# A two-layer graph network with routed experts: row terms turned by VectorE, layer-1 scaling on ScalarE, variance arithmetic on GpSimd, and another order within the steps

## The chip, the core and the metric

The kernel runs on one core of a Trainium2 chip. A core has five engines that work side by side, each through its own list of instructions in order: TensorE (PE in the profile; its weight loads are shown apart as PEld), VectorE (DVE), ScalarE (ACT), GpSimd (POOL) and SyncE (SP), which here only starts transfers. They meet through semaphores. TensorE writes into PSUM, which this kernel cuts into 8 banks of 512 fp32 values per partition; VectorE and ScalarE read PSUM and SBUF; the transfers with row indices (scatters) are started by GpSimd. The metric is the device time of one execution, in microseconds. Three runs of the kernel before gave a median of 1763.73 us (1761.31 to 1763.85).

## What is computed

There are 64 batches of 256 rows with 256 features, fp32 throughout, and one 256x256 adjacency that all batches share. Cut to what matters:

```python
x = x + elu(gat(layernorm(x), adj, W0, a0))       # 4 heads of 64, leaky slope 0.2
x = x + layernorm(x) @ Wf.T + bf
x = x + relu(gat(layernorm(x), adj, W1, a1))      # 1 head of 256, slope 0.01
t = layernorm(x)                                  # tokens
x = x + t + moe(t)                                # 8 experts, top 2, exact gelu, 256 -> 256 -> 256

def gat(h, adj, W, a):                            # per head
    q = h @ W
    e = leaky_relu(q @ a_src [rows] + q @ a_dst [columns])
    return softmax(where(adj, e, -big)) @ q
```

A batch therefore has four normalisations (call them norm 0, 1, 2 and 3: of the input, after layer 0's attention, after the linear layer, after layer 1's attention), two attentions, and a mixture of experts over all 16384 tokens.

## The kernel before, in words

**Attention without a softmax over scores.** The exponent of a leaky sum is written as a maximum of products, so one attention needs only, for each row, the exponentials of a few projected columns. `gnn_weights` (L139) widens the weight matrix by three columns per head: one for each of two terms along the keys and one for the term along the queries. `projected` (L322) multiplies the transposed input by that matrix (128x268 results for layer 0: 4 heads of 67; 128x259 for layer 1), lets ScalarE take `Exp` of the three columns with the row's 1/std as scale (L337), and lets VectorE scale the 64 (or 256) values of each head by 1/std and by one of the exponentials (L341). `scores` (L347) needs the query's term along the free axis of every partition: for each head and each half of the rows TensorE transposes a column that is broadcast to 128x128 (L353), which leaves the row term on all partitions of a PSUM tile `pd`. VectorE then forms `z = max(pd, key term) * mask` (L360). `attended` (L366) multiplies `z` by `q`, which has a column of sums at its end, and takes reciprocals.

**Normalisation.** `norm_stats` (L288) runs `bn_stats` and `bn_aggr` on VectorE for each half of a batch (L300, L301). `finish_norms` (L306) then makes 1/std on GpSimd in two instructions, an addition of eps (L308) and a power of -1/2 (L309). Two norms that fall into the same step share one pair of GpSimd instructions (tiles of 4 columns instead of 2).

**The order of the work.** The order is written out by a planner in the kernel (L909 to L942); nothing reorders it later. Every batch is a generator, `batch_layers` (L384), cut by `yield` into segments. A new batch begins every third step (`TICKS = 3`), and in each step every active batch issues one segment. Within a step the segments are issued by rank, lowest first; the rank of a segment is the number in the `yield` before it (or the one given to `begin`). So the work of one period (three steps, one new batch) holds one segment of every kind, each of another batch:

| step of the period | segments by rank, in the kernel before |
|---|---|
| first | relu of layer 1 (5), heads 2 and 3 of layer-0 scores (10), layer-1 projection (20), norm 1 and transposition (30), norm 0 and transposition of a new batch (40), tokens `xe` and `base` (50), second expert matmul `py`/`y` (80) |
| second | scaling of the experts' result (2), layer-1 scores (10), layer-0 projection (20), transposition of tokens (35), expert input `px` (40), layer-0 attention (50), norm 3 (60), linear layer and norm 2 (70), routing (75) |
| third | heads 0 and 1 of layer-0 scores (10), `by` from norm 3 (15), elu and residual (20), first expert matmul `ph` (30), layer-1 attention (40), router logits `pl` (50), transposition for layer 1 (60), routing (75) |

Norms 0 and 1 share GpSimd's two instructions in the first step ("finish A" below), norms 2 and 3 in the second ("finish B"). The order of issue is the order of every engine's list. All PSUM tiles come from one ring of 8 banks (`bank`, L78), so that no engine can be more than eight tiles ahead of the reader of the oldest.

**Experts.** Routing is done for chunks of four batches (later two and one): VectorE ranks tokens (`route`, L772), GpSimd sends each token's row to its two experts' regions in DRAM (L755, 4 indirect transfers per batch), and full pairs of 128 rows are loaded back, run through `expert_pair` (L598), and added into the output by GpSimd with accumulating indirect transfers (L695, 2 per pair, one pair per step, each waiting for the pair before it to land). In the middle of the run there are about two pairs per period; a period's pairs go 2, 2, 1, 3 over four batches. After the last batch the rest of the pairs and one batch done densely (`dense_expert`, L709) follow. Scatters and sends stand on GpSimd's list between finish A and finish B.

The lines in front of the change are these:

## Time and profile before

| what | value |
|---|---|
| median of three runs | 1763.73 us |
| the profiled execution | 1771.5 us, span 1769.8 us |
| TensorE busy (matmul) / weight loads | 1584.4 us (90%) / 1394.4 us (79%) |
| VectorE busy | 1296.0 us (73%) |
| ScalarE busy | 834.6 us (47%) |
| GpSimd busy | 838.8 us (47%) |
| mean granted TensorE clock | 0.957 |

A row of the profile's table of groups has the line, the engine, the operation, "output<-inputs", the number of instructions, the busy time, the mean duration, and the idle time of that engine just before them with the instruction that ended it. An fp32 matmul shows as two instructions. In the timeline a row has the start in us from the span's start, the duration, the engine, the line and the count of merged instructions; the bracket names an idle time before it and its releaser. Durations of neighbours overlap, since each includes the pipeline's tail: what an instruction takes from its engine is the distance between two starts. The starts of the linear layer's matmuls (L422), one group per batch, give the length of a period: 16.7 us where there is no expert work and no routing (from 113.6 us on, with longer ones between where a chunk is routed; 14 periods in the 263.8 us from 78.50 to 342.25 us), and a repeating 22.6, 23.5, 22, 26.1 us in the middle (43 periods in the 1023.3 us from 390.41 to 1413.73 us, 23.8 us each). The last 356 us hold two more periods and then experts alone.

The rows that the change touches, from the table of groups kept apart by shape:

| instruction | count | mean ns | busy us |
|---|---|---|---|
| L353 transposition of a broadcast column, PE | 640 | 280 | 105.3 |
| L341 scaling of `q`, 128x256, DVE | 256 | 479 | 112.6 |
| L300 `bn_stats`, DVE | 512 | 408 and 395 | 156.5 and 50.5 |
| L301 `bn_aggr`, DVE | 512 | 182 | 93.2 |
| L308 addition of eps, 128x4, POOL | 124 | 321 (median 228) | 39.7 |
| L309 power, 128x4 / 128x2, POOL | 124 / 8 | 1046 / 752 | 129.7 / 6.0 |

### The profile page before, as it was taken

To read this page: it belongs to the slowest core of one execution; us is meant where nothing else is said; L and a number is where in the kernel's file an instruction comes from. 1 tells how busy PE (TensorE), PEld (TensorE's weight loads), DVE (VectorE), ACT (ScalarE), POOL (GpSimd) and SP (SyncE) were. 2 spreads that over 40 slices of the span, in tenths; PEclk is the share of its full clock that TensorE was granted. 3 is DMA by queue.
4 is the path that set the end of the run, shared out by engine and by line. 5 is a ranking of instruction groups with operands and counts; after the bars stand their busy time and mean duration, and the time that the engine had idled before them with its cause. 6 is when DMAs were issued, how large, how long until landed. Compare 5 with 4: busy or idle time off the path is not lost. (4 is left out here: it accounts for less than half of the span.)

```text
span 1769.8 us, 29975 instructions
## 1 busy us (share of the span) xinstructions
PE 1584.4 (90%) x9254; PEld 1394.4 (79%) x9254; DVE 1296.0 (73%) x4808; ACT 834.6 (47%) x1773; POOL 838.8 (47%) x788
## 2 busy tenths in 40 slices
PE   5898889899999999999999999999999997688791
PEld 4777777688888888888888888888878886577681
DVE  6888888978787888878787878788888777422231
ACT  1232324255555555555555555555555565433340
POOL 0111333426555464646464646465664555634444
PEclk9999999999999999999999999999999898898896
DMA  3510112135545353544444444445453545665753
GB/s 101 173 37 24 54 50 68 53 108 116 131 111 134 90 127 101 126 115 123 118 110 123 94 118 111 130 111 136 116 133 84 111 120 133 173 180 96 172 110 42
DMA packets 137372, 192.89 MB, mean 109 GB/s; under 512 B 18680, under 2 KB 91392, under 8 KB 137216
## 3 DMA queue, kind: packets, MB, share of 16 engines
q1 hardware_dynamic: 86592, 122.61, 22.3%
q0 software_dynamic: 49632, 67.39, 20.7%
q8 instruction: 76, 1.25, 0.3%
q10 hardware_dynamic: 992, 0.99, 0.2%
q14 instruction: 80, 0.66, 0.1%
HBM read 101.77 MB, written 89.15 MB: 108 GB/s over the span
## 5 line engine op out<-in xcount | busy, mean ns | idle before, releaser
L695 POOL DMA_INDIRECT out_dram<-y,to x262 | 418.9, 1599 | 325.7 <-DMA out_dram<-y,to 150.1
L374 PE MATMUL pv<-q,z 128*128 128x65 f32 (+1 forms) x2560 | 366.3, 298 | 8.0 <-DVE y L684 8.0
L374 PEld LDWEIGHTS pv<-q,z 128*128 128x128 f32 x2560 | 337.2, 195 | 23.4 <-DVE y L684 10.0
L329 PE MATMUL pq<-wx,xT 128*128 128x268 f32 (+1 forms) x1024 | 269.2, 407 | 35.2 <-ACT xT L319 35.2
L663 PE MATMUL ph<-sT,we 128*128 128x256 f32 x1048 | 250.6, 395 | 46.3 <-ACT sT L635 25.5
L308 POOL TENSOR_SCALAR rstd<-mv 128x4 f32<-128x4 f32 (+1 forms) x132 | 43.4, 329 | 518.0 <-DVE mv L301 450.0
L755 POOL DMA_INDIRECT xs<-xng,pos x248 | 250.7, 1011 | 69.1 <-issue 67.7
L360 DVE SCALAR_TENSOR_TENSOR z<-pd,q,mask 128x256 f32<-128x256 f32 x640 | 265.1, 473 | 6.5 <-PE pd L353 6.3
L678 PE MATMUL py<-w2s,hT 128*128 (+1 forms) x1176 | 264.1, 380 | 0.6 <-ACT hT L669 0.6
L663 PEld LDWEIGHTS ph<-sT,we 128*128 128x128 f32 x1048 | 204.2, 200 | 76.1 <-ACT sT L635 27.1
L329 PEld LDWEIGHTS pq<-wx,xT 128*128 128x128 f32 x1024 | 191.0, 197 | 84.1 <-ACT xT L319 56.3
L678 PEld LDWEIGHTS py<-w2s,hT 128*128 128x128 f32 x1176 | 219.6, 190 | 28.6 <-ACT hT L669 1.0
L319 ACT COPY xT<-pt 128x512 f32<-128x512 f32 x256 | 143.6, 591 | 173.5 <-PE pt L315 173.5
L684 DVE TENSOR_TENSOR y<-py,b2s 128x512 f32<-128x512 f32 x147 | 97.3, 688 | 143.4 <-PE py L678 86.7
L656 ACT ACTIVATE y<-y,w 128x256 f32<-128x256 f32 x262 | 113.5, 498 | 187.9 <-DVE y L684 187.9
L669 ACT ACTIVATE hT<-ph,we 128x256 f32<-128x256 f32 x294 | 123.2, 470 | 164.6 <-PE ph L663 124.1
L341 DVE SCALAR_TENSOR_TENSOR q<-pq,rstd,q 128x256 f32<-128x256 f32 x256 | 112.6, 479 | 77.1 <-ACT q L337 76.9
L300 DVE BATCH_NORM_STATS2 stats<-x 128x6 f32<-128x256 f32 x384 | 156.5, 408 | 2.2
L309 POOL TENSOR_TENSOR rstd<-rstd,mhalf 128x4 f32<-128x4 f32 (+1 forms) x132 | 135.7, 1028 | 10.9
L422 PE MATMUL pf<-wfT,xT 128*128 128x256 f32 x512 | 132.0, 403 | 0.0
L353 PE MATMUL pd<-ident,q 128*128 128x128 f32 x640 | 105.3, 280 | 10.5 <-ACT q L337 10.5
L408 ACT ACTIVATE e<-hp 128x512 f32<-128x512 f32 x64 | 40.3, 630 | 155.9 <-DVE hp L402 155.9
(147 smaller groups left out, 2107.4 us busy)
## 6 DMA issues: line engine op xcount, KB each, us to landing
we<-wpack SPq DMA_DIRECT2D x147, 288.0 KB, 5.6
xr<-xs SPq DMA_DIRECT2D x131, 260.0 KB, 3.6
xin<-in_x_dram SPq DMA_DIRECT2D x64, 256.0 KB, 4.4
out_dram<-base SPq DMA_DIRECT2D x64, 256.0 KB, 3.4
out_dram<-y,to POOLq DMA_INDIRECT x262, 3.9
xs<-xng,pos POOLq DMA_INDIRECT x248, 2.6
xs<-fill SPq DMA_DIRECT2D x9, 260.0 KB, 5.0
wpack<-wt SPq DMA_DIRECT2D x8, 288.0 KB, 2.8
```

The costliest lines, as they stand in the source:

```text
L300: nc.vector.bn_stats(stats[:, t, :], src[:, t, :])
L309: nc.gpsimd.tensor_tensor(rstd[:, :n], rstd[:, :n], mhalf[:, :n], ALU.pow)
L319: nc.scalar.copy(dst, pt)
L329: nc.tensor.matmul(pq.rearrange("p h c -> p (h c)"), xT[:, k, t * P : (t + 1) * P], wx[:, k, :], start=(k == 0), stop=(k == KT - 1),)
L360: nc.vector.scalar_tensor_tensor(z[:, j, :], pd[:, i, :], q[:, j, h, d + 2 : d + 3], mask[:, j, :], op0=ALU.max, op1=ALU.mult,)
L374: nc.tensor.matmul(pv[:, h, :], z[:, j, t * P : (t + 1) * P], q[:, j, h, : d + 1], start=(j == 0), stop=(j == NT - 1),)
L422: nc.tensor.matmul(pf[:, t, :], xT[:, k, t * P : (t + 1) * P], wfT[:, k, :], start=(k == 0), stop=(k == KT - 1),)
L663: nc.tensor.matmul(ph[:, f, :], we[:, k * D + f * P : k * D + (f + 1) * P], xT[:, k, :], start=(k == 0), stop=(k == KT - 1),)
L669: nc.scalar.activation(hT[:, f, :], ph[:, f, :], AF.Gelu, bias=we[:, C_B1 + f : C_B1 + f + 1])
L678: nc.tensor.matmul(py[:, t, :], hT[:, f, t * P : (t + 1) * P], w2s[:, e, f * D : (f + 1) * D].rearrange("p e c -> p (e c)"), start=(f == 0 ...
L695: d = nc.gpsimd.indirect_dma_start(out=out_rows, out_offset=bass.IndirectOffsetOnAxis(ap=to[:, t : t + 1], axis=0), in_=y[:, t, :], in_off ...
L755: d = nc.gpsimd.indirect_dma_start(out=xs_d[: E * CAP * PAIR, :], out_offset=bass.IndirectOffsetOnAxis(ap=at, axis=0), in_=xe, in_offset=None,
```

## The change

There are four edits.

1. **Row terms of layer 0.** TensorE's eight transpositions per batch go. In the segment of the projection VectorE spreads each row's term over four columns, one per block of 32 partitions, with a mask `quad` (`quadrants`); in the third step one matmul with a constant `peers` (its ones join partitions with the same place in their block of 32) puts, on every partition, the term of the row at the same place of each block (`shared`, PSUM tile `pr`), and VectorE copies that to SBUF (`rs`). VectorE then transposes in blocks of 32x32 from `rs`, broadcast 32 times, straight into the PSUM tile `pd` (128x512, one instruction per two heads). The rest of `scores` is as before. Layer 1 keeps its two transpositions.
2. **Layer 1's projection.** `projected1` and `scores1` take the place of `projected` and `scores`: ScalarE scales the values (two `Copy` with the row's 1/std, out of PSUM), and multiplies the mask by the key's exponential (two `Copy` of 128x256, tile `me`), which VectorE then uses in place of the mask.
3. **Statistics.** VectorE's `bn_aggr` goes. GpSimd makes the variance from the even and odd halves of `bn_stats`: seven instructions instead of two in each finish, and an eighth for the doubled mean in the second step's.
4. **Order.** The new batch's segment gets rank 15 instead of 40, layer 1's projection 40 instead of 20, and `by` 45 instead of 15. On TensorE the first step then runs: transposition of the input, transposition after norm 1, layer-1 projection. Four work tiles lose their second buffer.

```diff
+    G = P // S                                   # S = 32
+    quad = const.tile([P, G], F32, tag="quad", name="quad")
+    nc.vector.tensor_reduce(quad, ident.rearrange("p (g a) -> p g a", a=S), AX.X, ALU.add)
+    peers = const.tile([P, G, S], F32, tag="peers", name="peers")
...
     def norm_stats(src):
...
-            nc.vector.bn_stats(stats[:, t, :], src[:, t, :])
-            nc.vector.bn_aggr(mv[:, at + t, :], stats[:, t, :])
+            nc.vector.bn_stats(stats[:, at + t, :], src[:, t, :])
...
     def finish_norms(n):
-        nc.gpsimd.tensor_scalar_add(rstd[:, :n], mv[:, :n, 1], EPS)
-        nc.gpsimd.tensor_tensor(rstd[:, :n], rstd[:, :n], mhalf[:, :n], ALU.pow)
+        nc.gpsimd.tensor_tensor(diff, stats[:, :, 1], stats[:, :, 4], ALU.subtract)
+        nc.gpsimd.tensor_tensor(rstd, stats[:, :, 2], stats[:, :, 5], ALU.add)
+        nc.gpsimd.tensor_tensor(diff, diff, diff, ALU.mult)
+        nc.gpsimd.tensor_scalar(diff, diff, D / 4.0, None, op0=ALU.mult)
+        nc.gpsimd.tensor_tensor(rstd, rstd, diff, ALU.add)
+        nc.gpsimd.tensor_scalar(rstd, rstd, 1.0 / D, EPS, op0=ALU.mult, op1=ALU.add)
+        nc.gpsimd.tensor_tensor(rstd, rstd, mhalf[:, :n], ALU.pow)
+        if (len(order_steps) - 1) % TICKS == 1:
+            nc.gpsimd.tensor_tensor(means, stats[:, :, 1], stats[:, :, 4], ALU.add)
...
+    def projected1(xT, rstd, b):
...
+        for t, pq in enumerate(pqs):
+            nc.scalar.activation(ex[:, t, :], pq[:, D:], AF.Exp, scale=rstd[:, t : t + 1])
+            nc.scalar.activation(q[:, t, :D], pq[:, :D], AF.Copy, scale=rstd[:, t : t + 1])
+        for j in range(NT):
+            nc.scalar.activation(me[:, j, :], masks[1][:, j, :], AF.Copy, scale=ex[:, j, 0:1])
...
+    def quadrants(q):
+        nc.vector.tensor_tensor(rq, <q's row terms, broadcast to G>, <quad, broadcast>, ALU.mult)
...
+    def shared(rq):
+        nc.tensor.matmul(pr, peers, rq, start=True, stop=True)      # 128x128 by 128x32
+        nc.vector.tensor_copy(rs, pr)
...
     def scores(q, heads, hs, mask, probs, rs=None):
+        if rs is not None:
+            nc.vector.transpose(pd, rs[:, heads of hs, :, None].to_broadcast([P, 2, NT * G, S]))
-        for i, h in enumerate(hs):
+        for i, h in enumerate(hs if rs is None else ()):
             ...transpositions by TensorE...
...
-        yield 20
-        q = projected(xT, wx1, 1, rstd)
+        yield 40
+        q, ex, me = projected1(xT, rstd, b)
...
-        yield 15
+        yield 45
         by = ...
...
-                    begin(nxt, 40)
+                    begin(nxt, 15)
```

## The prediction, as it was put on record

> **What bounds the kernel now.** The page comes first: engine totals, and the busy tenths of 40 slices.
>
> ```profile
> PE 1584.4 (90%) x9254; PEld 1394.4 (79%) x9254; DVE 1296.0 (73%) x4808; ACT 834.6 (47%) x1773; POOL 838.8 (47%) x788
> ...
> PE   5898889899999999999999999999999997688791
> ...
> DVE  6888888978787888878787878788888777422231
> ```
>
> TensorE is full from slice 8 to slice 32, but not in slices 2 to 7, where VectorE stands as high; so I read two stretches apart, by busy time per window (PE, PEld, DVE, ACT, POOL).
>
> ```profile
> 78.50:342.25 263.75, 229.19 (x1399) 196.24 (x1398) 228.95 (x809) 90.85 (x217) 70.48 (x89) 0.95 0.15 47
> ...
> 390.41:1413.73 1023.32, 988.95 (x5989) 883.66 (x5988) 837.69 (x3092) 566.04 (x1175) 573.24 (x526) 0.98 0.47 115
> ```
>
> The middle holds 43 periods of 23.8 us; TensorE works 23.0 of them (97%), VectorE 19.5, ScalarE 13.2, GpSimd 13.3. It is bound by TensorE's work. What stalls it, from the waits of TensorE between 400 and 1300 us (38 periods):
>
> ```profile
> PE pq L329 <- ACT xT L319: 15.2, 45, 0.6
> PE pv L374 <- DVE y L684: 6.4, 10, 0.7
> PE px L631 <- DMA xr<-xs: 5.9, 5, 2.2
> ```
>
> So 0.4 us per period is the layer-1 projection, which waits for a transposed tile that ScalarE is still copying. The early stretch (14 periods) differs: both engines are at 87%. One of its periods, TensorE:
>
> ```profile
> 208.63 0.60 PE L353 MATMUL pd<-ident,q 128*128 128x128 f32 x4
> 209.07 1.90 PE L374 MATMUL pv<-q,z 128*128 128x257 f32 x8
> 210.81 0.95 PE L489 MATMUL pl<-rT,xT 128*128 128x8 f32 x8
> 211.62 0.63 PE L315 MATMUL pt<-ident,x 128*128 128x128 f32 x4
> 212.09 0.60 PE L353 MATMUL pd<-ident,q 128*128 128x128 f32 x4
> 212.98 2.02 PE L329 MATMUL pq<-wx,xT 128*128 128x259 f32 x8 [0.29 <-ACT xT L319]
> ```
>
> and the next one's VectorE, GpSimd and ScalarE:
>
> ```profile
> 219.55 0.39 DVE L300 BATCH_NORM_STATS2 stats<-xin 128x6 f32<-128x256 f32 x1
> 219.98 0.18 DVE L301 BATCH_NORM_AGGREGATE mv<-stats 128x2 f32<-128x6 f32 x1
> 220.08 0.84 DVE L360 SCALAR_TENSOR_TENSOR z<-pd,q,mask 128x256 f32<-128x256 f32 x2
> 222.02 0.88 DVE L341 SCALAR_TENSOR_TENSOR q<-pq,rstd,q 128x256 f32<-128x256 f32 x2 [1.10 <-ACT q L337]
> ...
> 220.33 0.23 POOL L308 TENSOR_SCALAR rstd<-mv 128x4 f32<-128x4 f32 x1 [2.21 <-DVE mv L301]
> 220.64 1.04 POOL L309 TENSOR_TENSOR rstd<-rstd,mhalf 128x4 f32<-128x4 f32 x1
> ...
> 221.71 0.43 ACT L337 ACTIVATE q<-pq,rstd 128x12 f32<-128x12 f32 x2 [2.07 <-POOL rstd L309]
> ```
>
> VectorE idles 1.1 us there: the chain statistics, finish A on GpSimd, ScalarE's `Exp`, scaling of `q` has nothing behind it. Whatever makes finish A longer lengthens this period.
>
> **The change, part by part**, per batch (one period), costs as distances between starts.
>
> *TensorE.* Four transpositions take 0.44 us (208.63 to 209.07), so the eight removed are worth 0.88. The `peers` matmul (128x32, two passes) is nearest to `pl`: eight passes in 0.81 us, 0.10 each, so 0.2; between 0.2 and the 0.47 of two 128x268 passes. Net 0.66 less. `pr` stands directly after `pf`, where the first transpositions stood, but needs VectorE's scaling and mask (0.88 + 0.2 us) beyond `Exp`. In the middle this is covered: TensorE has token transposition, `px`, 3.5 us of layer-0 `pv` and 1.8 us of `pf` in between.
>
> *Order on TensorE.* The input's transposition and norm 1's (0.44 each) now stand between the layer-1 transposition and its projection, where 0.44 us of removed `pd` stood. The 0.4 us wait goes. The new batch's segment also issues the load of a later input; on SyncE's list it keeps its place, and on GpSimd's list no scatter or send changes sides with a finish. `by` moves behind layer 1's reciprocals, so that the longer finish B is waited for by nothing else on VectorE. Late next is layer 1's own `pd`: it waits for `Exp`, which on ScalarE now stands behind two copies `xT` (1.07 us in the middle's rows) and a scaling (0.42), on VectorE behind the extra work before layer 1's reciprocals. Its cover is `py`, 1.73 us per expert pair. With two or three pairs that holds; with one (a quarter of the periods) I expect about 1 us of wait, 0.25 per period.
>
> *VectorE.* Removed: layer 1's scaling, 0.78 (217.16 to 217.94 in that period); eight `bn_aggr`. A half of a batch now takes 0.53 us with aggregation; statistics alone should space like other 256-wide instructions (four `z` in 1.57 us, 0.39 each), 0.14 less, 1.1 per batch; at most 1.46 (the 93.2 us of L301 over 64). Added: two block transpositions of 128x512. No row shows this operation. Nearest are the 512-wide copy out of PSUM (L127, 684 ns) and addition into SBUF (L684, 688 ns): I take 0.69 each; below by two 128x256 at 0.39, no gain; above by twice the row, 1.38. `rq` and `rs` are small tiles (L786, 128x64 from PSUM, 192 ns): 0.2 each. Sum 1.78 - 0.78 - 1.1 = -0.1: VectorE's load stays.
>
> The Trainium skill's page "VectorE: DVE Perf Modes", section "The three transpose paths", speaks against this edit: it gives VectorE 311 ns for 128x128 in bf16, in 32x32 blocks only, and SBUF as the target. By that, as an estimate, four times 311 ns make 1.24 us per instruction, 1.1 us more per batch than my row, some 15 us over the early stretch; no run here shows it yet.
>
> *ScalarE.* Two scalings out of PSUM (like L445, a pair in 0.84) and two of the mask (like L656, four in 1.71): 1.7 us more on 13.2 of 23.8. The number of table loads in its list is unchanged. Alone it binds nothing; its place ahead of tokens delays layer 0's `Exp` by about as much as VectorE's experts' results already do.
>
> *GpSimd.* Per finish five more instructions, an eighth in B: eleven per period. A `tensor_scalar` on 128x4 starts the next 0.31 us later (220.33 to 220.64). The others are two-input instructions; their only row is the power, 752 ns on two columns and 1046 on four, which leaves 0.46 fixed, 0.54 with the gap. So 0.31 to 0.54: finish A grows by 1.55 to 2.5 us, a period by 3.4 to 5.9. I take 0.31 to 0.35, as additions are nearer to the addition than to a power. With its 0.3 us issue gaps GpSimd stands at 15.1 of 23.8, so at 18.5 to 21. Queued behind a finish are a period's four sends and the scatters; they lose idle time (450 us were spent waiting for statistics), and the experts' rows are needed a whole step later.
>
> The Trainium skill's "GPSIMD Engine Reference" (section "Elementwise — side-by-side cycle accounting") holds GpSimd about half as fast as VectorE for two-input work. Against it: here eight `bn_aggr` cost VectorE 1.1 us of spacing, and eleven GpSimd instructions cost 3.4 us of an engine that is 56% busy. By the rule statistics belong on VectorE, and the sum would be 20 us better early and about 1 us per period tighter in the middle.
>
> *Early stretch.* VectorE's order there is statistics, layer 1's two `z` (0.84), scaling of `q`. From the end of statistics to the scaling: finish A 2.9 to 3.7, `Exp` and hand-overs 0.5, less the 0.84. Against 1.1 before, idle time grows by 1.55 to 2.5, work shrinks by 0.1. So +1.4 per period, 14 periods, +20 us (at most +35; nothing, if ScalarE's new work and GpSimd's overlap better than I read). TensorE's removed work gives nothing here.
>
> *Middle.* VectorE 19.4, plus the wait for finish A behind results (1.3) and `z` (0.84), 1.2 to 2.0: about 21, under TensorE's 22.3. So TensorE stays the bound: -0.66 - 0.40 + 0.25 = -0.81 on 47 periods (43 and two at either end): -38 us.
>
> *Rest.* `quad` and `peers` are five small instructions in the set-up, under 1 us each: at most +1, among waits for weights. The smaller rings: each of the tiles is read out within two steps, and written once per three; nothing. The last 310 us (chain of waits: experts' matmuls and scatters that wait for each other) hold no edited instruction: 0.
>
> Sum: +20 - 38 + 1 = -17. The profiled execution took 1771.5 us, 0.4% over the median; 1754 for it, and 1746 for the median of runs. A measurement of this kernel can tell about 0.2%, 3.5 us.
>
> **Rivals.**
>
> *The vector chain takes the bound in the middle (slower).* If the block transposition costs 1.24 us or more, or GpSimd's instructions space at 0.54, VectorE's 21 becomes 22.1 to 23.5 and routing (10.6 us of VectorE instructions per four batches, unevenly placed) no longer fits. From 23.8 per period the middle gains nothing; early +1.4 to +2.5 remains. For it: VectorE's 82% plus a wait that lengthens. Against: over 4 us between 19.5 and 23.8 now. 1764 + 20 to 35: about 1785.
>
> *The early loss does not come.* If finish A's chain is hidden (statistics of the input now come first, and short GpSimd instructions may run closer than 0.31), only the middle counts: 1764 - 38 = 1726; with every stall gone too (0.8 + 0.66 on 47) 1695. Against it: the 1.1 us wait with GpSimd as releaser, 14 times.
>
> *Nothing moves.* TensorE's freed time turns into waits for the ring of 8 banks (`pv` already waits for `y`, and `pr` is one tile more): the middle gains 0.4, 1764 - 19 + 20 = 1765.
>
> **How the numbers follow.** Forecast (1730 to 1757): 0.37. No early loss (1695 to 1730): 0.27. Nothing moves (within 0.2%): 0.08. Vector chain (1768 to 1800): 0.28. Faster is the first two, 0.62 rounded down for the edge; slower 0.30. The range for 8 in 10 is 1708 to 1788; the forecast's own is 1730 to 1757.
>
> **What would show it.** Right: no L353-like row but the two layer-1 transpositions; block transposition near 0.69 us; GpSimd's small instructions near 0.3; middle periods near 23.0; early plain periods near 18.1 with VectorE waiting over 2 us for `Exp`; TensorE's wait for `xT` gone from the middle and a shorter one for layer 1's `Exp`. Wrong: a block transposition above 1.2 us, finish A above 4 us, TensorE below 92% in the middle, or early periods at 16.7.

## The result, and the profile after

The changed kernel takes 1821.97 us (median; 1809.02 to 1826.34), the kernel before beside it 1763.79 (1761.31 to 1768.47): a ratio of 1.0314, 95% interval 1.0254 to 1.0374. It is 3.1% slower, where 1746 us was forecast. The profiled execution took 1826.34 us, span 1824.6, to be set against the 1771.5 and 1769.8 of before.

The page of the changed kernel, engine totals and the busy tenths of 40 slices:

```profile
PE 1572.9 (86%) x8870; PEld 1382.3 (76%) x8870; DVE 1268.8 (70%) x4429; ACT 933.8 (51%) x2029; POOL 1007.8 (55%) x1516
...
PE   5888778789898989899999999899989987787792
...
DVE  6777888867678777868786868788778875422221
...
PEclk9889888889899999999999999999989999788896
```

All work that was to shrink did: TensorE has 384 instructions fewer, VectorE is busy 27 us less. But TensorE's slices 8 to 32, a row of nines before, now have eights among them, and the granted clock shows eights in the early slices, where it showed nines. The two stretches by themselves, same periods as before (14 early, 43 in the middle), busy time per window (PE, PEld, DVE, ACT, POOL, then the granted clock):

```profile
85.92:366.19 280.27, 228.76 (x1314) 197.35 (x1314) 224.55 (x725) 113.83 (x273) 106.07 (x244) 0.88 0.14 44
420.05:1460.27 1040.22, 968.66 (x5731) 863.46 (x5730) 815.25 (x2830) 630.72 (x1346) 683.46 (x997) 0.98 0.46 113
```

| stage, profiled execution | before | after | difference |
|---|---|---|---|
| start to the third linear layer | 78.5 | 85.9 | +7.4 |
| early, 14 periods | 263.8 (18.84 each) | 280.3 (20.02) | +16.5 |
| between | 48.2 | 53.9 | +5.7 |
| middle, 43 periods | 1023.3 (23.80 each) | 1040.2 (24.19) | +16.9 |
| rest | 356.1 | 364.3 | +8.3 |

No single stage carries the loss. Dividing a window's busy time by its periods gives two splits that the rest of this text uses. Early, VectorE was busy 16.36 us of a period and idle 2.49; it is now busy 16.04 and idle 3.98. In the middle TensorE was busy 23.00 and idle 0.80; it is now busy 22.53 and idle 1.66. TensorE did lose 0.47 us of work per period there, and waits 0.86 us more. What it waits for, in the middle window of the kernel before (total us, number, longest):

```profile
PE pq L329 <- ACT xT L319: 17.0, 50, 0.6
...
PE pv L374 <- DVE y L684: 8.0, 11, 1.6
...
PE px L631 <- DMA xr<-xs: 6.5, 6, 2.2
```

and in that of the changed kernel, with VectorE's longest wait above them:

```profile
DVE q L362 <- ACT q L358: 106.4, 43, 7.1
...
PE pt L336 <- DVE x L503: 27.7, 22, 2.4
...
PE pq L350 <- DVE z L449: 18.5, 11, 2.5
PE px L721 <- DMA xr<-xs: 17.9, 19, 2.4
```

The wait for `xT` is gone, as the new order promised. In its place TensorE waits for VectorE's residual `x1` (norm 1's transposition, 0.64 us per period), for a bank whose reader is VectorE's `z` (0.43), and longer for the experts' rows (0.42 after 0.15). VectorE's wait for layer 0's `Exp` has gone from 51.1 us in this stretch to 106.4.

**An early period.** TensorE, then VectorE, in the timeline of the changed kernel:

```profile
207.78 0.60 PE L336 MATMUL pt<-ident,xin 128*128 128x128 f32 x4
212.06 0.91 PE L336 MATMUL pt<-ident,x 128*128 128x128 f32 x4 [3.69 <-DVE x L503]
212.76 3.36 PE L382 MATMUL pq<-wx,xT 128*128 128x259 f32 x8
...
218.88 3.68 PE L463 MATMUL pv<-q,z 128*128 128x65 f32 x32
```

```profile
208.09 0.73 DVE L436 STREAM_TRANSPOSE pd<-rs 128x512 f32<-128x512 f32 x1
208.86 1.66 DVE L449 SCALAR_TENSOR_TENSOR z<-pd,q,mask 128x256 f32<-128x256 f32 x4
...
211.22 0.69 DVE L503 SCALAR_TENSOR_TENSOR x<-e,x 128x512 f32<-128x512 f32 x1
...
219.73 0.88 DVE L362 SCALAR_TENSOR_TENSOR q<-pq,rstd,q 128x256 f32<-128x256 f32 x2 [1.64 <-ACT q L358]
...
222.61 0.18 DVE L470 RECIPROCAL rinv<-pv 128x4 f32<-128x4 f32 x1 [1.60 <-PE pv L463]
```

TensorE waits 3.69 us for `x1`; then the layer-1 projection, which took 2.02 us in each of the 14 early periods before, takes 3.36 (3.1 to 3.7 in 12 of the 14 now); then VectorE waits for the `pv` behind it. Each waits for the other once per period, so a period is VectorE's work plus its waits. The two waits over the whole early stretch, in the kernel before and in the changed kernel:

```profile
DVE q L341 <- ACT q L337: 14.1, 14, 1.1
PE pt L315 <- DVE x L412: 13.4, 6, 3.5
...
PE pt L336 <- DVE x L503: 44.4, 14, 5.7
...
DVE q L362 <- ACT q L358: 25.3, 13, 2.9
```

**A middle period.** GpSimd's list from finish B to finish A in the changed kernel:

```profile
1049.89 0.20 POOL L321 TENSOR_TENSOR diff<-stats 128x4 f32<-128x4 f32 x1 [1.58 <-DVE rs L428]
...
1052.39 0.62 POOL L330 TENSOR_TENSOR double<-stats 128x4 f32<-128x4 f32 x1
1053.17 1.55 POOL L845 DMA_INDIRECT xs<-xng,pos  x1 [0.17 <-issue]
...
1060.75 1.58 POOL L785 DMA_INDIRECT out_dram<-y,to  x1 [0.30 <-ACT xng L553]
1061.77 0.80 POOL L321 TENSOR_TENSOR diff<-stats 128x4 f32<-128x4 f32 x1
...
1063.83 1.04 POOL L328 TENSOR_TENSOR rstd<-rstd,mhalf 128x4 f32<-128x4 f32 x1
```

and VectorE beside it:

```profile
1057.74 0.74 DVE L311 BATCH_NORM_STATS2 stats<-x 128x6 f32<-128x256 f32 x2
...
1065.21 0.88 DVE L362 SCALAR_TENSOR_TENSOR q<-pq,rstd,q 128x256 f32<-128x256 f32 x2 [5.05 <-ACT q L358]
```

The statistics for finish A are there at 1058.5, but GpSimd reaches them only at 1061.77: between the two finishes it has four sends and two scatters and no idle time but the gap at each issue. VectorE stands for 5.05 us. The counterpart before has the same four sends and two scatters, ends them at 972.2 and has 1.42 us to spare:

```profile
961.95 0.23 POOL L308 TENSOR_SCALAR rstd<-mv 128x4 f32<-128x4 f32 x1 [12.26 <-DVE mv L301]
962.26 1.04 POOL L309 TENSOR_TENSOR rstd<-rstd,mhalf 128x4 f32<-128x4 f32 x1
...
970.60 1.60 POOL L695 DMA_INDIRECT out_dram<-y,to  x1 [0.30 <-issue]
973.62 0.22 POOL L308 TENSOR_SCALAR rstd<-mv 128x4 f32<-128x4 f32 x1 [1.42 <-DVE mv L301]
```

The two periods are not quite alike: in the one before VectorE also routes tokens ahead of these statistics (some 3 us, from 965.98 to 968.96), in the changed kernel's it does not. The mean over all 43 middle periods says the same without this. From the end of its last statistics to the first instruction of finish A it takes 0.30 us in the kernel before (over 0.3 us in 10 periods) and 1.66 us in the changed kernel (in 31); finish A itself takes 1.53 and 3.07 us there. In the early stretch, where there are few sends, the delay is 0.15 and 0.10 us, and finish A takes 1.34 and 2.54.

### The profile page after: what moved, and what is told of

It is laid out like the page before. It is cut to its first block, busy times and chain, and to the rows that moved or that the text cites. A ratio compares the mean times of both kernels' runs of the same rounds, so it can differ in the third digit from the quotient of the medians.

```text
span 1824.6 us, 29624 instructions
## 1 busy us (share of the span) xinstructions
PE 1572.9 (86%) x8870; PEld 1382.3 (76%) x8870; DVE 1268.8 (70%) x4429; ACT 933.8 (51%) x2029; POOL 1007.8 (55%) x1516
## 5 line engine op out<-in xcount | busy, mean ns | idle before, releaser
L845 POOL DMA_INDIRECT xs<-xng,pos x248 | 265.1, 1069 | 67.6 <-issue 66.7
L753 PE MATMUL ph<-sT,we 128*128 128x256 f32 x1048 | 254.9, 400 | 42.3 <-ACT sT L725 21.6
L321 POOL TENSOR_TENSOR diff<-stats 128x4 f32<-128x4 f32 (+1 forms) x132 | 59.0, 447 | 383.3 <-DVE stats L311 309.3
L449 DVE SCALAR_TENSOR_TENSOR z<-pd,q,mask 128x256 f32<-128x256 f32 x512 | 212.4, 478 | 4.5
L336 PE MATMUL pt<-ident,x 128*128 128x128 f32 x512 | 88.5, 300 | 88.3 <-DVE x L503 87.6
L362 DVE SCALAR_TENSOR_TENSOR q<-pq,rstd,q 128x256 f32<-128x256 f32 x128 | 56.3, 481 | 147.7 <-ACT q L358 147.7
L382 PE MATMUL pq<-wx,xT 128*128 128x259 f32 x512 | 156.8, 460 | 0.9 <-ACT xT L340 0.9
L350 PE MATMUL pq<-wx,xT 128*128 128x268 f32 x512 | 133.5, 402 | 19.9 <-DVE z L449 18.5
L311 DVE BATCH_NORM_STATS2 stats<-x 128x6 f32<-128x256 f32 x384 | 142.7, 414 | 2.2
L336 PEld LDWEIGHTS pt<-ident,x 128*128 128x128 f32 x512 | 64.9, 160 | 98.2 <-issue 52.1
```

The lines of the kernel that those rows point to most:

```text
L311: nc.vector.bn_stats(stats[:, at + t, :], src[:, t, :])
L336: nc.tensor.transpose(pt[:, k, t * P : (t + 1) * P], src[:, t, k * P : (k + 1) * P], ident)
L350: nc.tensor.matmul(pq.rearrange("p h c -> p (h c)"), xT[:, k, t * P : (t + 1) * P], wx[:, k, :], start=(k == 0), stop=(k == KT - 1),)
L382: nc.tensor.matmul(pq, xT[:, k, t * P : (t + 1) * P], wx1[:, k, :], start=(k == 0), stop=(k == KT - 1),)
L449: nc.vector.scalar_tensor_tensor(z[:, j, :], pd[:, i, :], q[:, j, h, d + 2 : d + 3], mask[:, j, :], op0=ALU.max, op1=ALU.mult,)
L753: nc.tensor.matmul(ph[:, f, :], we[:, k * D + f * P : k * D + (f + 1) * P], xT[:, k, :], start=(k == 0), stop=(k == KT - 1),)
```

## The experiments

Every ratio is against the kernel before on the same chip, with its 95% interval. Waits, periods and busy times are from each kernel's profiled execution; the kernel before differs by 1.0% between the chips (medians 1764 to 1781 us), so microseconds of different runs are compared roughly. "Delay of finish A" is the mean time from its last statistics to its first instruction in the 43 middle periods.

### One edit undone

**proj20**: the layer-1 projection goes back in front of the two transpositions.

```diff
-        yield 40
+        yield 20
         q, ex, me = projected1(xT, rstd, b)
```

> The changed kernel, with one rank put back: layer 1's projection at 20 instead of 40, so that TensorE runs it between the input's transposition and norm 1's transposition. Theory 'order' (TensorE stalls because norm 1's transposition now stands ahead of the projection and meets VectorE's residual x1 too early, 87.6 us of waits against 18.8 before, and works at a lower clock after each stall): the waits for x1 fall below 30 us and the time to 1745 to 1775. Theory 'GpSimd' (finish A is late because GpSimd's list is longer, VectorE waits 147.7 us for layer 0's Exp against 76.9): the waits for x1 may fall, but VectorE's waits stay near 150 us and the time at 1805 or more.

Measured: 1.0436 [1.0332, 1.0539]. The wait for `x1` leaves the top of TensorE's list, and that for a bank that `z` reads grows from 18.5 to 25.3 us, `xT` returns with 14.1, and the experts' rows stay (27.6 after 29.2). Early periods are 19.97 us, middle ones 24.56 instead of 24.19, with less idle time (1.45 after 1.66) but TensorE busy 23.12 instead of 22.53, at a granted clock of 0.96 instead of 0.98. That the new rank is what made the kernel slow falls.

**order_back**: all three ranks as before.

```diff
-                    begin(nxt, 15)
+                    begin(nxt, 40)
...
-        yield 40            # layer-1 projection
+        yield 20
...
-        yield 45            # by
+        yield 15
```

> The changed kernel with all three ranks as before (40, 20, 15); the other three edits stay. 'Order': 1755 to 1785, a little slower than with one rank put back, since the projection's wait for the copied tile (15 to 20 us in all) returns and `by` now waits for finish B on VectorE. 'GpSimd': 1810 to 1850, since the norms of the input are again taken after norm 1 and `by` waits for a finish B that is 2 us longer.

Measured: 1.0387 [1.0312, 1.0463]; early periods 21.31 us instead of 20.02, the start 93.7 us instead of 85.9. Beside the other edits the new order is not what costs; that it gains there is not shown, since the two intervals overlap.

**aggr_back**: `bn_aggr` on VectorE and finishes of two GpSimd instructions again.

```diff
-            nc.vector.bn_stats(stats[:, at + t, :], src[:, t, :])
+            nc.vector.bn_stats(stats[:, t, :], src[:, t, :])
+            nc.vector.bn_aggr(mv[:, at + t, :], stats[:, t, :])
...
-        nc.gpsimd.tensor_tensor(diff, stats[:, :, 1], stats[:, :, 4], ALU.subtract)
-        ...seven more...
+        nc.gpsimd.tensor_scalar_add(rstd[:, :n], mv[:, :n, 1], EPS)
+        nc.gpsimd.tensor_tensor(rstd[:, :n], rstd[:, :n], mhalf[:, :n], ALU.pow)
```

> The changed kernel with the aggregation back on VectorE and the two-instruction finish on GpSimd; the other edits stay. 'GpSimd': VectorE's wait for layer 0's Exp falls from 147.7 to about 80 us, the time to 1765 to 1790. 'Order': VectorE has 1.1 us more per period ahead of x1, TensorE's waits for x1 stay at 87 us or grow, the time is 1815 to 1850.

Measured: 1.0137 [1.0065, 1.0209], 1.7% less than the changed kernel. The waits of the whole run:

```profile
PE pt L326 <- DVE x L493: 90.7, 40, 5.9
...
DVE q L352 <- ACT q L348: 65.5, 65, 3.2
```

VectorE's wait for `Exp` falls from 147.7 to 65.5 us; TensorE's for `x1` stays (87.6 before the undoing). The delay of finish A falls from 1.66 to 0.38 us. So these are two losses. Most of the gain is in the middle (23.56 us per period instead of 24.19); early periods are even longer (20.45 instead of 20.02), because VectorE has its 1.35 us of aggregation back.

**rows_back**: TensorE transposes layer 0's row terms again.

```diff
-        rq = quadrants(q)
...
-        rs = shared(rq)
-        scores(q, H, range(0, 2), masks[0], probs, rs)
+        scores(q, H, range(0, 2), masks[0], probs)
```

> The changed kernel with layer 0's row terms transposed by TensorE again; the other edits stay. 'Order' and 'GpSimd': TensorE gets back 0.66 us per period, which lies on a period that TensorE's stalls and work set together: 1820 to 1860. A third theory, 'VectorE' (the two block transpositions and two small tiles, 1.8 us per period ahead of x1 and of the statistics, are what makes x1 late): x1 is 1 us earlier in each period, TensorE's waits for x1 fall by half, 1780 to 1800.

Measured: 1.0231 [1.0134, 1.0328]. The mirror image: the start is back at 79.2 us and early periods at 18.41, below the kernel before, but the middle is 24.56. Its waits:

```profile
DVE q L362 <- ACT q L358: 202.2, 65, 7.5
...
PE pt L336 <- DVE x L501: 43.5, 26, 4.9
PE px L719 <- DMA xr<-xs: 41.0, 41, 3.0
```

With less work of its own VectorE has the statistics ready earlier, but finish A starts 2.77 us after them (1.66 in the changed kernel), so it waits longer for `Exp`, 3.1 us each time.

**act_back**: layer 1's scaling on VectorE, `projected` and `scores` as before.

```diff
-        q, ex, me = projected1(xT, rstd, b)
+        q = projected(xT, wx1, 1, rstd)
...
-        z = scores1(ex, me)
+        probs = []
+        scores(q, 1, range(1), masks[1], probs)
```

> The changed kernel with layer 1's scaling and mask product taken from ScalarE: VectorE scales the values again, as before; the other edits stay. If ScalarE's longer list (two scalings and two mask products ahead of the tokens and of layer 0's Exp, 1.7 us per period) is part of the loss, the time falls to 1790 to 1810 and VectorE's wait for layer 0's Exp with it. If it is not, VectorE has 0.78 us more per period ahead of the statistics and the time is 1825 to 1850.

Measured: 1.0359 [1.0314, 1.0405], against 1.0314 with the edit: ScalarE's part does no harm, as forecast.

### One edit alone, on the kernel before

**only_order** has the three new ranks alone, **only_stats** the statistics on GpSimd alone, **only_rows** the row terms on VectorE alone; the diffs are the parts of the change shown ahead of the prediction. All three, and order_act below, keep the changed kernel's single buffers of four work tiles, whose price by themselves no run here isolates.

> The kernel before with the three ranks changed and nothing else (apart from the smaller buffers). If the order alone helps by what putting it back cost in the changed kernel (20 us): 1735 to 1755. If TensorE's earlier need of x1 (its norm-1 transposition ahead of the projection) costs more than the projection's wait saved: 1770 to 1800.

> The kernel before with GpSimd's statistics alone: five more GpSimd instructions in each finish, as in the kernel with the long finish, but VectorE is relieved of the aggregation (1.1 us per period) and the two-input instructions follow each other faster than multiplications do. If the length of the finish is what costs (98 us for 1.55 us of it), a finish that is 1.2 us longer costs 75 us, less at most 50 us for VectorE's relief: 1785 to 1830. If VectorE's load is what counts, the relief wins: 1740 to 1765.

> The kernel before with the row terms of layer 0 alone moved to VectorE (and the changed kernel's single buffers); aggregation, layer-1 scaling and ranks are as before. Theory 'two stretches' (the row terms cost VectorE 1.8 us per period where VectorE is the bound, and give TensorE 0.66 where TensorE is): the early stretch grows by 25 us and the set-up by 5 to 10, the middle shrinks by 20 to 28 us, together 1765 to 1785. If TensorE's freed time is worth nothing in the middle: 1790 to 1810.

Measured: ranks 1.0116 [1.0080, 1.0153], statistics 1.0207 [1.0170, 1.0243], row terms 1.0438 [1.0400, 1.0475]. Each is slower; together (with ScalarE's scaling) they cost 1.0314, less than the row terms alone. The row terms were forecast far too cheap on both theories. Where they hit in the old order (waits of the whole run):

```profile
PE pq L340 <- ACT xT L330: 56.5, 82, 1.0
PE pq L340 <- DVE z L433: 49.7, 25, 4.3
```

TensorE waits for a bank that VectorE's `z` has yet to read, a wait that the kernel before has nowhere among its larger ones. In the middle TensorE is busy 22.55 us of a period instead of 23.00 and idle 2.07 instead of 0.80.

**order_act** is the other half of the change: new ranks and ScalarE's scaling, with row terms and statistics as before.

```diff
-                    begin(nxt, 40)
+                    begin(nxt, 15)
...
-        q = projected(xT, wx1, 1, rstd)
+        q, ex, me = projected1(xT, rstd, b)
```

> The changed kernel without VectorE's row terms and without GpSimd's statistics: what is left are the new ranks and layer 1's scaling on ScalarE. Undoing both harmful edits at once: if they add up (8 us for the row terms and 27 us for the statistics, each undone alone), 1780 to 1795. If VectorE's chain was loaded beyond its margin by both, so that taking both away frees more than the sum, the early stretch falls to 16.8 to 17.8 us per period, the middle to 23.2 to 23.6, the time to 1725 to 1755, faster than before.

Measured: 0.9955 [0.9924, 0.9985], slightly faster than the kernel before. With the ranks alone it was 1.0116, so under the new order, without the other two edits, ScalarE's scaling gains some 1.6%. These two edits are not where the loss is, and they make one kernel of a square: order_act (0.9955), with row terms added (aggr_back, 1.0137), with statistics added (rows_back, 1.0231), with both (the changed kernel, 1.0314). By its profiled executions, per period:

| kernel | early | VectorE busy + idle | middle | TensorE busy + idle | start |
|---|---|---|---|---|---|
| order_act | 18.77 | 15.60 + 3.18 | 23.79 | 22.98 + 0.81 | 77.7 |
| + row terms | 20.45 | 17.39 + 3.07 | 23.56 | 22.35 + 1.22 | 88.9 |
| + statistics | 18.41 | 14.31 + 4.11 | 24.56 | 23.22 + 1.34 | 79.2 |
| + both | 20.02 | 16.04 + 3.98 | 24.19 | 22.53 + 1.66 | 85.9 |

The middle windows behind it, of order_act, with row terms and with statistics (that of both stands above):

```profile
389.29:1412.24 1022.95, 988.22 (x5988) 888.15 (x5988) 802.09 (x3006) 629.47 (x1347) 583.98 (x525) 0.98 0.47 115
...
420.84:1434.05 1013.21, 960.86 (x5730) 858.15 (x5730) 872.84 (x3178) 628.95 (x1347) 581.97 (x526) 0.98 0.47 116
...
392.19:1448.22 1056.03, 998.51 (x5988) 892.85 (x5988) 752.19 (x2662) 629.82 (x1347) 689.99 (x997) 0.97 0.46 112
```

Early and at the start the row terms cost, mostly through VectorE's busy time; in the middle the statistics cost, through waits: VectorE has 1.2 to 1.3 us less work per period with them and 1.9 to 2.0 us more idle time. Executions of one kernel differ by up to 1.5% (1838 to 1866 us for proj20; 1809 to 1826 for the changed kernel), some 0.36 us on a middle period. So the statistics' 0.77 and 0.63 us there are to be read; the row terms' gain of 0.23 and 0.37 is at the edge.

### The length of the finish

**finish_long**: the kernel before, with five multiplications by 1.0 in each finish.

```diff
         nc.gpsimd.tensor_scalar_add(rstd[:, :n], mv[:, :n, 1], EPS)
+        for _ in range(5):
+            nc.gpsimd.tensor_scalar(rstd[:, :n], rstd[:, :n], 1.0, None, op0=ALU.mult)
         nc.gpsimd.tensor_tensor(rstd[:, :n], rstd[:, :n], mhalf[:, :n], ALU.pow)
```

> The kernel before with five more small GpSimd instructions in each finish (a multiplication by 1.0 of the same tile, each depending on the last), nothing else. It puts the length of the finish alone on the chip, 1.5 us more each time. Theory 'GpSimd' (the length of the finish, on a list that sends and scatters share, delays layer 0's Exp): early +1.5 per period (20 us), middle +0.4 to 0.8 per period (17 to 35 us), 1800 to 1820. If the loss by the new finish lies in something else (what VectorE meets when both engines work on the statistics, say), 1764 to 1785.

Measured: 1.0565 [1.0521, 1.0609], +98 us, twice what was expected. No other engine got any work. Whole run:

```profile
DVE q L343 <- ACT q L339: 157.6, 83, 6.3
...
DVE by L456 <- POOL rstd L311: 89.0, 47, 10.0
```

In the kernel before these are 76.9 and 21.5 us: in the old order VectorE pays for both finishes, A at `q` and B at `by`. Together +148 us, more than the 98 us that the kernel lost. Early periods grew from 18.84 to 21.23 us, as VectorE's idle time did (2.49 to 4.79); middle ones grew from 23.80 to 24.81. A finish takes 2.88 us instead of 1.35 to 1.5, so two of them are 3.1 us longer per batch, and about half of that, 98 us over 64 batches, was lost. The expectation had counted A alone. So the latency of a finish is on VectorE's path in the kernel before already.

### Amount of VectorE work, or its place

**load**: order_act with three more VectorE instructions per batch whose result is not read.

```diff
+    def extra(n):
+        t = work.tile([P, 4, P], F32, tag="extra", name="extra", bufs=2)
+        m = masks[0].rearrange("p a (b c) -> p (a b) c", c=P)
+        nc.vector.tensor_tensor(t[:, :n], m[:, :n], m[:, :n], ALU.mult)
...
         q = projected(xT, wx0, H, rstd)
+        extra(NT)
...
+        extra(2 * NT)
         scores(q, H, range(0, 2), masks[0], probs)
...
+        extra(2 * NT)
         scores(q, H, range(2, 4), masks[0], probs)
```

> The kernel before with the new ranks and ScalarE's scaling of layer 1 (0.9955 of the kernel before), plus three VectorE instructions per batch whose result nobody reads, two of 128x512 ahead of the z of layer 0 and one of 128x256 behind the scaling of q: about 0.7 + 0.7 + 0.4 us, what the row terms add on VectorE, at the same places. TensorE keeps its transpositions, its tiles and its ring. Theory 'amount': the row terms' price is VectorE's time; early periods go from 18.8 to 20.2 or more and the time to 1.010 to 1.025 of the kernel before. Theory 'coupling': the price comes from the row terms' path (VectorE to TensorE to VectorE, one more tile in the ring of banks, tiles written by VectorE); then this load alone costs little: early periods under 19.5, 0.995 to 1.005.

Measured: 1.0149 [1.0113, 1.0185] where order_act has 0.9955 and the row terms on order_act 1.0137. The windows of the load:

```profile
84.50:360.50 276.00, 228.24 (x1399) 198.24 (x1397) 238.50 (x823) 113.19 (x273) 75.14 (x90) 0.93 0.15 45
408.40:1437.50 1029.10, 991.28 (x5989) 890.75 (x5988) 867.89 (x3135) 629.25 (x1347) 591.23 (x525) 0.98 0.47 114
```

1.76 us of VectorE work per batch (673 ns twice, 415 once) cost 1.9% without any new PSUM tile, matmul or handover between engines: early periods 19.71 instead of 18.77, the start 84.5 us instead of 77.7. So 'coupling' falls as the whole price: up to the end of the early stretch the load costs 20 us, where the row terms cost 35 (aggr_back against order_act). The amount of work is a little over half of it. Early periods miss the 20.2 that 'amount' asked for, and with the row terms they are 0.75 us longer still (VectorE 0.35 busier, 0.4 more idle); what that rest is stays open. In return the row terms have the shorter middle, where TensorE's work is gone. There the load's 1.53 us of VectorE work per period cost only 0.14 us (23.93 after 23.79): VectorE's idle time took it up.

**x1_first** and **z_late** move VectorE's scores in the changed kernel, one behind `x1`, one behind the statistics, into the wait for finish A; **both_moved** has both.

```diff
-        yield 10            # heads 0 and 1            (x1_first, both_moved)
+        yield 25
...
-        yield 10            # heads 2 and 3            (z_late, both_moved)
+        yield 35
```

> The changed kernel with one number altered: the segment of layer 0's heads 0 and 1 gets rank 25 in the third step instead of 10, so that VectorE makes the residual x1 first. Nothing is left out. Theory 'circle': in the early stretch the period is a circle of VectorE (hp to x1) and TensorE (norm 1's transposition, layer-1 and layer-0 projection, pv), each waiting for the other; the copy of the row terms, one block transposition and four z (0.2 + 0.73 + 1.6 us) stand on it ahead of x1. Off it, early periods fall from 20.0 to 17.5 to 18.5, the wait of TensorE for x1 (87.6 us) falls under 30, and the time is 1780 to 1800. Theory 'load': the added VectorE work counts wherever it stands; early periods stay at 19.5 to 20.5 and the time at 1810 to 1830.

> The changed kernel with one number altered: the segment of layer 0's heads 2 and 3 gets rank 35 in the first step instead of 10, so that one block transposition and four z (2.4 us of VectorE) stand behind the statistics of norms 0 and 1, where VectorE otherwise waits for finish A and the Exp behind it. Nothing is left out. Theory 'finish A is waited for': the cover takes most of that wait; VectorE's wait for Exp falls from 148 to under 80 us, the middle from 24.2 to 23.5 to 23.8 per period, and the time is 1780 to 1800. Theory 'GpSimd's list': finish A stands behind scatters and sends, so earlier statistics are not finished earlier; the wait stays above 120 us and the time at 1810 to 1830.

> The changed kernel with both numbers altered (rank 25 for heads 0 and 1, 35 for heads 2 and 3). Nothing is left out. If 'circle' and 'finish A is waited for' hold and belong to different stretches, the gains add: 1745 to 1775. If both numbers only shift one wait to the other, it is no better than the better of the two: 1780 to 1830.

Measured: 1.0286 [1.0224, 1.0348], 1.0323 [1.0255, 1.0392] and 1.0385 [1.0333, 1.0437]; the changed kernel has 1.0314. Neither cure works. In x1_first the wait for `x1` is gone, and the same matmul waits elsewhere (whole run):

```profile
PEld pt L336 <- DVE z L449: 51.8, 35, 2.3
...
PE pt L336 <- DVE z L449: 44.1, 25, 2.1
...
PEld pt L336 <- DVE rs L428: 32.4, 21, 4.1
...
PE pt L336 <- DVE rs L428: 27.5, 20, 3.9
```

`z` and `rs` don't feed that transposition; in the kernel they read tiles of the ring whose banks it is to write next. With one ring of 8 banks, VectorE work that is put later holds TensorE by its banks instead of by its result. In z_late VectorE's wait for `Exp` falls only from 147.7 to 126.1 us: statistics that come earlier are not finished earlier, because sends and scatters stand ahead of finish A, as in the middle period above. The delay of finish A is 3.65 us here, after 1.66.

**oae_both** applies the same two numbers to order_act with the addition of eps on VectorE.

> The kernel before with the new ranks, ScalarE's scaling of layer 1 and the addition of eps on VectorE (TensorE's transpositions and bn_aggr on VectorE kept), and both numbers altered (rank 25 for heads 0 and 1, 35 for heads 2 and 3). Nothing is left out. If the circle and the wait for finish A also bind this kernel (VectorE's wait for Exp is 84 us without the two numbers, TensorE's for x1 55 us), it gains 10 to 35 us on 1761: 1725 to 1750, faster than both kernels. If TensorE's work binds it, nothing is gained: 1750 to 1765.

Measured: 1.0121 [1.0075, 1.0168], 1.8% worse than without the two numbers (0.9944, below). Covering these waits does not pay in this kernel either: middle periods are 24.44 us, 23.36 without the two numbers.

**pd_sbuf**: the block transposition writes to SBUF, outside the ring.

```diff
-        pd = bank("pd", [len(hs), N])
+        pd = work.tile([P, len(hs), N], F32, tag="pdS", name="pdS", bufs=2)   # row terms only
```

> The changed kernel with the block transposition's result in an SBUF tile of its own (two buffers) instead of a tile of the ring of 8 banks. Nothing is left out. Theory 'amount': no change, 1.025 to 1.035 of the kernel before. Theory 'ring': two tiles per batch fewer in the ring let TensorE run further ahead; its waits for z and rs go, and the time falls to 1.005 to 1.02.

Measured: 1.0259 [1.0218, 1.0301]; the interval overlaps that of the changed kernel (1.0254 to 1.0374). The transposition takes 706 ns instead of 724, early periods 19.44 us instead of 20.02, the middle is unchanged (24.24), and TensorE's wait for `x1` as well (92.2 us); its wait for the bank that `z` reads (18.5 us) is gone. So about half a per cent of the loss may lie in these tiles, which the intervals do not separate from none. The early gain came with a granted clock of 0.94 instead of 0.88 (TensorE busy 15.42 us of a period instead of 16.34, and no less idle), so it need not be the ring's.

### What is left of the change

**hybrid_aggr**: the changed kernel with aggregation on VectorE, and VectorE's row terms only from batch 16 on, that is in the middle alone.

```diff
-        rq = quadrants(q)
+        rq = quadrants(q) if b >= 16 else None
...
-        rs = shared(rq)
+        rs = shared(rq) if rq is not None else None
```

> The changed kernel with the aggregation back on VectorE and with VectorE's row terms only from batch 16 on, where expert work has begun; before that TensorE transposes them. 'Two stretches' and 'GpSimd' together: early stretch 18.0 to 18.6 us per period instead of 20.4, middle 23.5 as with the aggregation put back alone: 1755 to 1770. If the early loss does not come from the row terms: 1790 to 1800.

Measured: 1.0013 [0.9994, 1.0032]. Early periods are 19.17 us and middle ones 23.79, both above what was expected, but the profiled execution took 1782.7 us where the median is 1770.4. Keeping the row terms away from the early stretch is worth 22 us against aggr_back. But order_act, with no such row terms at all, has 0.9955: in the middle the 0.55 us per period that TensorE saves (22.43 busy instead of 22.98) come back as idle time (1.35 instead of 0.81), and both have 23.79 us periods. Since hybrid_aggr's profiled execution was 0.7% over its median, some 0.17 us of a period, a small gain there is not excluded.

**order_act_eps**: order_act with the addition of eps on VectorE, so that a finish is one GpSimd instruction.

```diff
-        nc.gpsimd.tensor_scalar_add(rstd[:, :n], mv[:, :n, 1], EPS)
+        nc.vector.tensor_scalar(rstd[:, :n], mv[:, :n, 1], EPS, None, op0=ALU.add)
         nc.gpsimd.tensor_tensor(rstd[:, :n], rstd[:, :n], mhalf[:, :n], ALU.pow)
```

> The same as the kernel with the new ranks and ScalarE's scaling alone, with the addition of eps moved from GpSimd to VectorE, so that a finish is one GpSimd instruction: 0.31 us shorter on GpSimd, one small VectorE instruction (about 0.1 to 0.17 us) more per finish. If the finish's length costs 98 us for 1.55 us, 0.15 to 0.2 us less is worth 5 to 15 us against that kernel; if hidden there, the two are within 5 us.

Measured: 0.9944 [0.9920, 0.9969], the fastest kernel here, though not to be told from order_act. It is faster than the kernel before and the changed kernel: the half of the change that was kept is worth about half a per cent.

## Why the prediction was wrong, point by point

**Durations: right.** The block transposition took 724 ns (0.69 taken). The Trainium skill's "VectorE: DVE Perf Modes" (section "The three transpose paths") had led to an estimate of 1.24 us; the measurement decides for the nearest rows. `bn_stats` alone spaces at 0.33 us (0.39 taken), so VectorE lost 27 us of work where 6 were forecast. GpSimd's small instructions start 0.15 to 0.32 us apart (0.31 to 0.35 taken); finish A is 2.5 us long after 1.35 in the early stretch, less than the +1.55 forecast, but 3.07 after 1.53 in the middle, where behind a scatter 0.72 us pass between its second and third instruction. TensorE's waits for `xT` went; layer 1's `pd` waits 1.0 us for `Exp` in the whole middle (0.25 per period forecast).

**Early stretch, +20: the size came out, its parts did not.** Measured +16.5. By the prediction's own split, VectorE's idle time grows by 1.49 us per period (1.55 forecast) and its work shrinks by 0.31 (0.1). But the idle time was to come from finish A alone, and the wait for `Exp` grew by 0.8 us per period. In the square the statistics make early periods shorter, by 0.36 and 0.43 us: the aggregation saved (-1.3) outweighs the idle time they add (+0.9). On the old order alone (only_stats) they make them 0.36 us longer. What lengthens them is the row terms, by 1.68 and 1.61, whose work (+1.7) the forecast had cancelled against the aggregation and layer 1's scaling (-0.76). That scaling came back as idle time: in order_act VectorE is idle 3.18 us instead of 2.49, in a period of 18.77 instead of 18.84. So the agreement in size is in part luck. Nor was it foreseen that TensorE's wait for `x1` joins in (44.4 us in the stretch after 13.4) and slows the projection behind it.

**Middle, -38: wrong, and this term decides.** Measured +16.9, that is +0.39 us per period where -0.81 was summed. The step that failed is "about 21, under TensorE's 22.3. So TensorE stays the bound". It gave the longer finishes no price in the middle and counted TensorE's removed work in full. By the square, per period: new order and ScalarE's scaling 0 (23.80 to 23.79; -0.15 summed); row terms -0.23, or -0.37 beside the statistics (-0.66 summed, though TensorE's work did shrink by 0.63 and 0.69); statistics +0.77, or +0.63 beside the row terms (0 summed). On either path they add up to +0.39. It was not the amount of VectorE's work that took the room between 21 and 23.8: the load put 1.53 us more into a middle period for 0.14. It was the finish: finish A starts 1.66 us after its statistics instead of 0.30 and takes 3.07 us instead of 1.53, and VectorE waits for `Exp` behind it (106.4 us after 51.1). TensorE's stalls did not go from 0.80 to 0.65 but to 1.66, as the sum (-0.47 + 0.86 = +0.39 per period) requires. Row terms brought the waits for `x1` and `z` (27.4 and 21.0 us in aggr_back's middle, 12.6 and none among the larger ones in order_act's), the statistics lengthened that for the experts' rows (25.3 in rows_back's middle, 12.5 in order_act's).

**GpSimd's queue: wrong.** "They lose idle time" was said of the sends and scatters behind a finish, because GpSimd waited 450 us for statistics in the whole run. That is an average over both finishes. In the middle of the kernel before GpSimd was idle 4.44 us ahead of a finish B, but only 1.00 us ahead of a finish A. In the period shown it had 1.42 us to spare there, and finish B, 3.1 us long after 1.35, used it up; in the changed kernel 0.19 us is left on average. "The experts' rows are needed a whole step later" fell with it: TensorE's wait for them grew from 6.5 to 17.9 us in the middle. That late sends are behind this wait was argued, not isolated.

**Rest: wrong.** "At most +1" for the set-up holds for its new constants, but the stage before the third linear layer also has the first periods, whose VectorE work is that of the early stretch: +7.4 us, and +6.8 for the load alone, which has no new constants. "0" for the last 310 us stands against +8.3 in the rest, which no run here takes apart; kernels with the longer finishes had 360 to 369 us there, those with short ones 353 to 361. That rest also holds the last two periods, so the zero for what comes after them is not tested.

**The rivals.** "The vector chain takes the bound in the middle" had the right sign and the wrong condition and price: it asked for a transposition of 1.24 us or a GpSimd spacing of 0.54, neither came, and the kernel went past its 1785 all the same, past 1800 and past the 1788 of the range for 8 in 10. "The early loss does not come" fell. "Nothing moves" named part of the mechanism, TensorE's freed time turning into waits for the ring, which cost more than the freed time.

**The weighing of GpSimd.** The Trainium skill's "GPSIMD Engine Reference" (section "Elementwise — side-by-side cycle accounting") was read as "statistics belong on VectorE", worth 20 us early and 1 us per period in the middle. Its direction was right: putting them back gains 1.7%. The place was the reverse: early periods get 0.43 us longer, middle ones 0.63 shorter. What cost there was the finish's length and its place on GpSimd's list; the rate per element no run here tests.

## What to carry to other kernels

An engine that is 97% busy is not therefore the only bound: if another in-order engine waits for it and is waited for by it once per period, take work off the first and ask, wait by wait, whether the second delivers any earlier. Spare time counted from averages took up extra work here (the load, in the middle) but not a longer wait for another engine. A few short instructions on the engine that also starts scatters can cost the whole kernel: 1.5 us in each of two finishes cost 1.5 us per batch. What is to be asked is how long that engine's list is between two finishes, not how idle it is overall. Before moving VectorE work out of the way of one wait, look at which PSUM banks it frees: the same matmul may be held there instead.

## What the hardware showed unexpectedly

After a wait of 3.69 us the eight-pass projection took 3.36 us, at a granted clock of 0.57. In 12 of the 14 early periods of the changed kernel it took 3.1 to 3.7 us at 0.50 to 0.60, each time shortly behind a wait of 2.32 us or more; in the other two it took 1.92 us at 1.00, behind 0.5 and 2.32 us. In the kernel before, with waits of at most 0.29 us just ahead, all 14 took 2.02 us at 1.00. So a part of a wait's price is paid after it, though a wait of 2.32 us was seen with either clock. Over the early stretch the granted clock fell from 0.95 to 0.88; with the row terms undone it was 0.95 again, but also 0.94 in pd_sbuf, whose waits for `x1` are as long and where seven of the 14 projections took 1.92 us.

In the middle the granted clock was 1.00 in the profiled execution of order_act_eps, 0.95 in the four kernels with moved scores, and 0.96 to 0.99 in the others; TensorE was 96 to 97% busy in order_act_eps and in oae_both alike. All four ran on one chip, the one on which the kernel before took longest (median 1781 us, though at a mean clock of 0.958, after 0.959 to 0.960 on the others). Whether the order or the chip sets it no run isolates.

`bn_stats` on 256 values starts every 0.33 us when two stand next to each other, though its row shows 0.41 us each; with `bn_aggr` behind each, a half-batch took 0.53 us. And a block transposition of 128x512 fp32 values, read from a tile broadcast 32 times, took hardly longer into PSUM (724 ns) or SBUF (706 ns) than a copy or an addition of that size (684 and 688 ns before).
